# Two hypernetwork convolutions: new layout for the small network's variances, merging on ScalarE, another kind of weights last in each step, another order of transfers

## The chip, the cores and the metric

The program runs on one core of a Trainium2 chip. The metric is the device time of one execution in microseconds (us). The profile is of one execution, and its rows name the engines PE (TensorE), PEld (TensorE's weight loads), DVE (VectorE), ACT (ScalarE), POOL (GpSimd) and SP (SyncE, which here only issues DMAs). L586 is line 586 of the kernel before.

## The reference

x has the shape (32, 32, 64, 256): 32 samples s, 32 batches b, 64 channels, 256 places l. Two layers of the same form follow each other, each with its own parameters:

```python
# GroupNorm of each sample: 32 groups of 8 places l, each over b, channels and its places
xn = (x - mean) / sqrt(var + 1e-5)
# a small network makes a convolution of its own for every (b, l)
h  = relu(LN(z @ W1 + b1))                       # (32, 256, 128)
w  = (h @ W2 + b2).reshape(32, 256, 64, 64, 3)   # in, out, tap
hb = relu(LN(z @ Wb1 + bb1))                     # a second one for the bias
bias = (hb @ Wb2 + bb2)
out[s,b,o,l] = sum_ik xn[s,b,i,l+k-1] * w[b,l,i,o,k] + bias[b,o,l]
x = x + out
```

The group's statistics of layer 2 are those of layer 1's result. LN is the LayerNorm over the 128 hidden values; since z has 16 columns, its variance is a quadratic form in z (the matrix is called `form` in the kernel).

## The kernel before

**Units and steps.** A layer is worked in 32 units (4 quarters of the 256 places x 8 groups of 4 b's), a unit in two halves of 32 output channels. So the kernel has 128 steps v. In step v PE makes the weights of half a unit in 12 groups: `make` (L574, L575) multiplies the hidden values by 8 output channels' part of W2 into a PSUM tile `pg` (three buffers). The three kinds of groups (0, 1, 2) are the pairs of taps. `take` adds b2 and puts the result into the SBUF tile `wall`, of which there is one: kinds 0 and 1 with one add of DVE (L586, 128 partitions), kind 2 with an add of DVE for 64 partitions (L586, 64x1024) and eight of ACT for the other 64 (L597, one for each channel). `order` in the program lists the twelve: four times the kinds 2, 0, 1.

**Products.** `products(v)` multiplies the normalized x (`xn`) by `wall` (L621, 288 matmuls in four quarters into `pc`, two buffers), and DVE adds each quarter to the residual in `ring` (L630). In layer 1 DVE then takes the statistics of the new x (`bn_stats`, L314, two for each quarter) for layer 2. PE's order is written out: the first group of step v+1 is made ahead of `products(v)`, the other eleven behind it. Since `wall` is one tile, `products(v)` waits for the last `take` of step v, and the first `take` of step v+1 for `products(v)`.

**Around a step.** `after(v)` issues the transfers on SP: in layer 1 the pieces of x for the statistics of the next quarters (`land`, L664), the store of the result (L523), the residual of step v+2 (L186), hidden values (L141), the next half of x into `raw` (L170 or L179), which POOL normalizes (L560, twice 128x2112 for each half) and the bias (L511, four DMAs), which POOL adds to the residual (L518). `agenda` spreads the rest over the twelve places k of a step: DVE's `bn_stats` of the pieces (L671), and, when a quarter's statistics are complete, their merging (`Merge`, L331 to L356: eight operations of DVE, a matmul `over` L342, four of DVE, a second matmul, a root on ACT, a reciprocal on DVE). `Table` spreads mean and root over the partitions.

**First phase.** Ahead of step 1 the kernel takes the statistics of the first 11 of 32 groups (22 transfers of 1 MB, `bn_stats` L476 on DVE), and in between works the small networks for all units: 16 `Unit`s, two (hidden and bias net) for each of 8 pieces of z. For each, PE forms and sums the quadratic form (L248, L253) with the positions on the free axis, ACT takes relu and root of 128x512 (L254, L255), DVE the reciprocal of 128x512 (L256) and POOL multiplies (L257); then PE makes the hidden values (L267), ACT brings them out (L269) and sends them to DRAM (L279), and the bias net's go through PE once more (L289) and out (L298, L305). The twelve groups of step 0 are put among the last units, then come the merging, the table and the normalization of unit 0 on DVE (L560).

Of the kernel before, what the change touches and what calls it, by code (L numbers as in the profile page):

```python
# [23 lines left out]
FP = mybir.dt.float32  # L24
# [6 lines left out]
P = 128  # L31
# [8 lines left out]
PARAMS = ("z", "wc", "vec", "W2", "b2", "Wb2")  # L40
# [3 lines left out]
def conv_layers(  # L44
# [40 lines left out]
    hd = [dram.tile([2, P, 2 * M], FP, name=f"hd_{i}") for i in range(U // 2)]  # L85
# [18 lines left out]
    apart = const.tile([P, G], FP, name="apart")  # L104
# [33 lines left out]
    def load_hidden(i):  # L138

        h = hp.tile([P, 2, 2, M], FP, tag="hT", name="hT")  # L140
        nc.sync.dma_start(  # L141
            out=h.rearrange("p b a m -> p b (a m)"), in_=hd[i].rearrange("b p f -> p b f")
        )
        for b in range(2):
            hs[2 * i + b] = h[:, b]
# [44 lines left out]
    class Network:  # L190


        def __init__(self, stage, par, n):
# [10 lines left out]
            self.form = stage.tile([P, 2, P], FP, name=f"form_{n}")  # L204
            nc.gpsimd.memset(self.form, 0.0)

        def prepare(self, stage):
# [5 lines left out]
            for net in range(2):  # L213
# [6 lines left out]
                for r in range(0, P, R):  # L220
                    x = slice(r, r + R)
                    nc.vector.tensor_scalar(self.form[x, net, x], p2[x, x], 1.0 / P, None, ALU.mult)

    class Unit:


        def __init__(self, nets, zts, blocks, e):
            self.e, self.blocks = e, blocks
            self.j, self.net = divmod(e, 2)
            self.w = nets[self.j * NR // (UL // 2)]  # L230
            self.zt = zts[self.j % 2]
            flat = xn.rearrange("p n t j s -> p (n t j s)")
            self.q = flat[:, e % 3 * BLK : (e % 3 + 1) * BLK]
            o = 3 * BLK
            if self.net:
                o += 6 * BLK
                self.ht = [flat[:, o + k * 2 * BLK : o + (k + 1) * 2 * BLK] for k in range(2)]
            else:
                self.ht = [flat[:, o + x * 2 * BLK : o + (x + 1) * 2 * BLK] for x in ((e + k) % 3 for k in range(2))]
            o = 13 * BLK  # L240
            self.bs = [
                flat[:, o + k * BLK // 2 : o + (k + 1) * BLK // 2].rearrange("p (t a m) -> p t a m", t=NT, a=2)
                for k in range(3)
            ]

        def project(self):
            p = ps_c.tile([P, BLK], FP, tag="pc", name="pt")
            nc.tensor.matmul(p, self.w.form[:, self.net], self.zt, start=True, stop=True)  # L248
            nc.vector.tensor_tensor(self.q, self.zt, p, ALU.mult)
# [612 lines left out]
```

## Time and profile before

| | |
|---|---|
| three runs | 4101.36, 4085.76 and 4092.62 us, median 4092.62 us |
| the profiled execution | 4084.62 us, of it 4082.8 us in the span of the profile |
| busy, share of the span | PE 94%, PEld 90%, DVE 67%, POOL 47%, ACT 31% |
| granted TensorE clock, mean | 0.974 of full speed |
| first phase, to the last evacuation of step 0 | 250.06 us |
| step 1 | 39.16 us |
| steps 2 to 64 (the rest of layer 1 and the first of layer 2) | 1953.76 us, PE busy 1845.27 us |
| from there to the end | 1839.82 us, PE busy 1802.65 us |

The end of a step is read throughout as the start of the fourth L630 of its products: the moment at which PE has finished the products. A busy share says how full an engine is over a whole stretch. It doesn't say which wait ends last in a step, for which the rows with their idle times are needed: in brackets behind a row stands how long the engine idled ahead of it and what it waited for. "issue" there means that nothing in the profile shows what it waited for.

### The profile page before, as it was taken

The page shows a single profiled execution, that of the slowest core. Times are in us where ns is not written, and L with a number is a line of the kernel's source. Part 1 is how long each engine was busy: PE and PEld are TensorE (multiplying, and loading weights), DVE is VectorE, ACT ScalarE, POOL GpSimd, SP SyncE. Part 2 cuts the span into 40 slices and gives each one's busy share as a digit, 9 for nine tenths or more (in the row PEclk, how much of TensorE's full clock was granted, in tenths as well). Part 3 has the DMA queues.
Part 4 walks back from the last instruction along what each step waited for, and adds up shares of the span by engine and source line. Part 5 has one row for each costly group of instructions (what it writes and reads, how often), then busy time and mean ns, then how long its engine had stood idle before and what let it go on. Part 6 is the DMA issues. An engine that isn't in the chain of part 4 may idle for free.

```text
span 4082.8 us, 185286 instructions
## 1 busy us (share of the span) xinstructions
PE 3824.2 (94%) x86444; PEld 3655.0 (90%) x86444; DVE 2715.9 (67%) x3019; ACT 1276.0 (31%) x4320; POOL 1935.0 (47%) x629
## 2 busy tenths in 40 slices
PE   5669999799998999899998999999999999999999
PEld 1369999799987999899998999999999999999999
DVE  5677777777777777767676556565656565656565
ACT  3423333233222333233332323233323233323232
POOL 1143554434544445535545446654555455545542
PEclk6789999899999999999999999999999999999999
DMA  6565655455554554444457877787877787878783
GB/s 235 158 232 178 200 176 172 140 185 187 182 182 133 187 183 161 141 129 155 149 153 174 153 141 158 143 161 148 156 141 155 142 160 146 156 147 157 143 153 93
DMA packets 655906, 657.74 MB, mean 161 GB/s; under 512 B 563736, under 2 KB 587680, under 8 KB 589216
## 3 DMA queue, kind: packets, MB, share of 16 engines
q1 hardware_dynamic: 629024, 633.31, 62.4%
q8 instruction: 676, 11.08, 1.2%
q10 hardware_dynamic: 26112, 12.59, 1.1%
q14 instruction: 94, 0.77, 0.1%
HBM read 496.91 MB, written 148.90 MB: 158 GB/s over the span
## 4 chain that ended last, share of the span: by engine, by line
PE 85%; DVE 10%; issue 2%; DMA 1%; ACT 1%; ACTq 1%; POOL 0%; SPq 0%; DVEq 0%; POOLq 0%
PE pg L574 55%; PE pc L621 23%; PE pg L575 5%; DVE wall L586 4%; DVE parts L314 1%; DVE ring L630 1%; PE pt L248 0%; DMA ring<-in_xg_dram 0%; DVE first_parts L476 0%; DVE parts L335 0%; DMA land<-in_xg_dram 0%; ACTq L305 0%; DVE parts L334 0%; ACT wall L597 0%; DVE xn L256 0%
## 5 line engine op out<-in xcount | busy, mean ns | idle before, releaser
L574 PE MATMUL pg<-hT,w2t 128*64 128x128 f32 x24576 | 2755.1, 274 | 80.8 <-DVE wall L586 74.1
L574 PEld LDWEIGHTS pg<-hT,w2t 128*64 128x64 f32 x24576 | 2690.0, 137 | 124.3 <-DVE wall L586 90.8
L575 PE MATMUL pg<-hT,w2t 128*64 128x128 f32 x24576 | 2755.5, 274 | 1.3 <-issue 1.0
L575 PEld LDWEIGHTS pg<-hT,w2t 128*64 128x64 f32 x24576 | 2690.2, 137 | 1.6 <-issue 1.4
L586 DVE TENSOR_TENSOR wall<-pg,b 128x1024 f32<-128x1024 f32 (+1 forms) x1536 | 1861.1, 1219 | 604.3 <-PE pg L575 599.5
L597 ACT ACTIVATE wall<-pg,b 64x128 f32<-64x128 f32 x4096 | 1161.7, 474 | 2655.2 <-DVE wall L586 1939.5
L560 POOL TENSOR_TENSOR xn<-raw,tab 128x2112 f32<-128x2112 f32 x126 | 664.0, 5270 | 1591.5 <-PE pc L621 1398.4
L621 PE MATMUL pc<-wall,xn 128*32 128x128 f32 (+1 forms) x36864 | 960.5, 262 | 67.9 <-issue 59.3
L621 PEld LDWEIGHTS pc<-wall,xn 128*32 128x32 f32 x36864 | 913.4, 110 | 116.4 <-issue 108.4
L630 DVE TENSOR_TENSOR ring<-pc,ring 128x512 f32<-128x512 f32 x512 | 353.9, 691 | 658.7 <-PE pc L621 643.7
L518 POOL TENSOR_TENSOR ring<-ring,bt 128x2048 f32<-128x2048 f32 x127 | 580.0, 4567 | 41.8 <-DMA bt<-bd 33.5
L560 POOL TENSOR_TENSOR xn<-xn,tab 128x2112 f32<-128x2112 f32 x126 | 592.0, 4698 | 9.9
L314 DVE BATCH_NORM_STATS2 parts<-ring 128x6 f32<-128x256 f32 x512 | 192.9, 418 | 8.7
L671 DVE BATCH_NORM_STATS2 first_parts<-land 128x6 f32<-128x512 f32 x168 | 114.4, 681 | 8.4 <-DMA land<-in_xg_dram 8.4
L257 POOL TENSOR_TENSOR xn<-xn,zt 128x512 f32<-128x512 f32 x16 | 20.3, 1266 | 155.0 <-DVE xn L256 134.3
L554 POOL COPY raw<-edge 64x64 f32<-64x64 f32 x96 | 28.6, 298 | 137.1 <-DMA edge<-xe 134.8
L398 POOL COPY tab<-spot 64x1024 f32<-64x1024 f32 x28 | 29.0, 1035 | 129.7 <-ACT spot L385 128.8
L256 DVE RECIPROCAL xn<-xn 128x512 f32<-128x512 f32 x16 | 53.6, 3350 | 25.0 <-ACT xn L255 25.0
L289 PE MATMUL pb<-xn,Wb 128*64 128x256 f32 x128 | 29.0, 562 | 37.4 <-ACT xn L298 33.8
L289 PEld LDWEIGHTS pb<-xn,Wb 128*64 128x64 f32 x128 | 8.9, 180 | 57.9 <-ACT xn L298 45.1
L269 ACT ACTIVATE xn<-ph,vec 128x1024 f32<-128x1024 f32 x32 | 37.5, 1198 | 24.0 <-PE ph L267 14.7
L476 DVE BATCH_NORM_STATS2 first_parts<-ring 128x6 f32<-128x512 f32 x68 | 41.2, 668 | 4.8 <-DMA ring<-in_xg_dram 4.8
(81 smaller groups left out, 399.3 us busy)
## 6 DMA issues: line engine op xcount, KB each, us to landing
bt<-bd SPq DMA_DIRECT2D x508, 256.0 KB, 6.1
raw<-in_xp_dram SPq DMA_DIRECT2D x63, 1056.0 KB, 10.0
ring<-in_xs_dram SPq DMA_DIRECT2D x64, 1024.0 KB, 8.2
x<-ring SPq DMA_DIRECT2D x64, 1024.0 KB, 4.9
raw<-x SPq DMA_DIRECT2D x256, 256.0 KB, 7.9
ring<-x SPq DMA_DIRECT2D x64, 1024.0 KB, 9.4
out_dram<-ring SPq DMA_DIRECT2D x64, 1024.0 KB, 4.9
land<-in_xg_dram SPq DMA_DIRECT2D x48, 1024.0 KB, 5.1
```

The costliest lines, as they stand in the source:

```text
L256: nc.vector.reciprocal(self.q, self.q)
L314: nc.vector.bn_stats(out, y.rearrange("p o (a m) -> p o a m", a=2)[:, :, :, g * e : (g + 1) * e])
L476: nc.vector.bn_stats(first_parts[:, g, bg], slots[order[i]][:, k])
L518: nc.gpsimd.tensor_tensor(y, y, bts.pop(v), ALU.add)
L560: eng.tensor_tensor(o, i, tab[:, x, None, j0:j1].to_broadcast(list(o.shape)), op)
L574: nc.tensor.matmul(pg[0:C, k, :], w[:, k0 * C : (k0 + 1) * C], h0, start=True, stop=True)
L575: nc.tensor.matmul(pg[C:P, k, :], w[:, k1 * C : (k1 + 1) * C], h1, start=True, stop=True)
L586: nc.vector.tensor_tensor(place(rows, a), pg[rows].rearrange("p o (t m) -> p t m o", t=NT), b2[n][rows, kind, None, None, o0 : o0 + OG].to ...
L597: nc.scalar.activation(place(rows, a)[:, :, :, k], pg[rows, k].rearrange("p (t m) -> p t m", t=NT), AF.Identity, bias=b2[n][rows, kind, o0 ...
L621: nc.tensor.matmul(pc[t * S : (t + 1) * S, n0 - q * EB : n1 - q * EB, :], xn[:, u % 2, t, p, :], wall[:, t, a : a + (n1 - n0) * CH], start ...
L630: nc.vector.tensor_tensor(part, pc.rearrange("p (m a) o -> p o a m", a=2), part, ALU.add)
L671: nc.vector.bn_stats(first_parts[:, g, bg], lands[i % LAND])
```

## The change

The diff below is cut to its core; every part that the prediction speaks of is in it.

1. **Variances with positions on partitions.** `Batch` takes the place of `Unit`: eight of them, each for both nets and four units. The variance of a position becomes one number on a partition's row, so relu, root and reciprocal work on 128x32 instead of 128x512, once for both nets. New are a second layout of z as an input (`zp`), two multiplications of 128x256 and a reduction on DVE, and eight transposes with a copy of 128x1024 on ACT (`turn`).
2. **First phase.** The 22 transfers come in the order of groups; the merging of the first 9 groups starts after 18 of them, and the last two groups are merged in step 2.
3. **Merging on ScalarE.** Of the eight operations of DVE three reductions stay; scaling and squaring go to ACT (`around`), the rest is folded into the second matmul. `Table.expand` goes to POOL and `spread` one step later.
4. **Order of kinds.** The twelve groups of a step are four times 0, 1, 2. The last two `bn_stats` of `products` come behind the first `take` of the next step.
5. **Transfers of a step.** The store stands first, then the pieces, the residual, the bias (a step earlier than before) and the hidden values; the half of x is issued at k = 2.
6. **Two buffers for x.** From unit 24 on the second half of a unit goes to `land` instead of `raw`.

```diff
     class Batch:
...
+        def variance(self):
...
+            for x in range(2):
+                nc.vector.tensor_tensor(
+                    q[:, x], t[:, x, :, :, 0:A], zp[:, x, :, None, :].to_broadcast([P, 2 * NR, 2, A]), ALU.mult
+                )
+            nc.vector.tensor_reduce(self.var, self.q.rearrange("p (y a) -> p y a", a=A), AX.X, ALU.add)
+            var = self.var.rearrange("p (x r n) -> p x r n", x=2, n=2)
+            nc.vector.tensor_tensor(var, var, t[:, :, :, :, A], ALU.add)
+            nc.scalar.activation(self.var, self.var, AF.Relu)
+            nc.scalar.activation(self.var, self.var, AF.Sqrt, bias=eps)
         def scale(self):
-            nc.scalar.activation(self.q, p, AF.Relu)
-            nc.scalar.activation(self.q, self.q, AF.Sqrt, bias=eps)
-            nc.vector.reciprocal(self.q, self.q)
-            nc.gpsimd.tensor_tensor(self.q, self.q, self.zt, ALU.mult)
+            nc.vector.reciprocal(self.var, self.var)
...
+        def turn(self):
...
+            nc.scalar.copy(self.zq, p)
...
-        def merge(self):
...
-            nc.vector.tensor_reduce(m, means, AX.X, ALU.add)
-            nc.vector.tensor_scalar(m, m, 1.0 / shape[2], None, ALU.mult)
-            nc.vector.tensor_reduce(v, squares, AX.X, ALU.add)
-            nc.vector.tensor_tensor(means, means, m[:, :, None].to_broadcast(shape), ALU.subtract)
-            nc.vector.tensor_tensor(means, means, means, ALU.mult)
-            nc.vector.tensor_reduce(d, means, AX.X, ALU.add)
...
+        def sums(self):
+            nc.vector.tensor_reduce(self.m, self.means, AX.X, ALU.add)
+            nc.vector.tensor_reduce(self.v, self.squares, AX.X, ALU.add)
+        def around(self):
...
+            nc.scalar.activation(self.v, self.v, AF.Copy, scale=1.0 / N1)
+            for g in range(self.n):
+                nc.scalar.activation(self.means[:, g], self.means[:, g], AF.Square, bias=self.d[:, g : g + 1])
+        def spans(self):
+            nc.vector.tensor_reduce(self.d, self.means, AX.X, ALU.add)
...
-                if n == 0:
-                    for g in range(2 * q, 2 * q + 2):
-                        bn_stats(parts[:, g, bg, h, :], y, g)
+                if n == 0 and q < NB - 1:
+                    last_stats(v, q)
...
+        def place_half(u, k):
+            return land if k == 1 and u >= 3 * BG else raw
...
         def after(v):
             u, h = divmod(v, NH)
+            store(v)
             load_pieces(v + 1)
-            store(v)
             if v + 2 < NH * U:
                 load_residual(v + 2)
+                load_bias(v + 2)
             if h == 1 and u % 2 == 1 and u + 3 < U:
                 load_hidden((u + 3) // 2)
-            next_half(*((u + 1, 1) if h == 0 else (u + 2, 0)))
-            if v + 1 < NH * U:
-                next_bias(v + 1)
         starts = range(0, CH, OG)
-        order = [(kind, o) for o in starts for kind in (2, 0, 1)]
+        order = [(kind, o) for o in starts for kind in (0, 1, 2)]
...
         def agenda(v):
             todo = {k: [] for k in range(len(order))}
+            u, h = divmod(v - 1, NH)
+            todo[0].append(lambda: last_stats(v - 1))
+            todo[0].append(lambda: after(v - 1))
+            todo[2].append(lambda: next_half(*((u + 1, 1) if h == 0 else (u + 2, 0))))
+            if v + 1 < NH * U:
+                todo[5].append(lambda: add_bias(v + 1))
...
             for m in merges:
-                todo[2].append(m.merge)
-                todo[4].append(m.mean)
-                todo[6].append(m.root)
+                todo[2].append(m.sums)
+                todo[3].append(m.around)
+                todo[5].insert(0, m.spans)
+                todo[6].append(m.mean)
+                todo[8].append(m.root)
```

The next rows are the instructions of DVE around the products of a step in layer 2, in the order in which the built program has them (`wall<-pg` is `take`'s add, `ring<-pc` the addition of the products). Before:

```order
L586 TENSOR_TENSOR wall_205<-pg_32545,b2_1_228 64x128x8
L586 TENSOR_TENSOR wall_205<-pg_32571,b2_1_228 128x128x8
L586 TENSOR_TENSOR wall_205<-pg_32589,b2_1_228 128x128x8
L630 TENSOR_TENSOR ring_204<-pc_32624,ring_204 128x64x8
L630 TENSOR_TENSOR ring_204<-pc_32662,ring_204 128x64x8
L630 TENSOR_TENSOR ring_204<-pc_32700,ring_204 128x64x8
L630 TENSOR_TENSOR ring_204<-pc_32738,ring_204 128x64x8
L586 TENSOR_TENSOR wall_205<-pg_32607,b2_1_228 64x128x8
```

And the same place of the changed program (L646 is the add, L697 the addition of the products):

```order
L646 TENSOR_TENSOR wall_205<-pg_33948,b2_1_228 128x128x8
L646 TENSOR_TENSOR wall_205<-pg_33966,b2_1_228 128x128x8
L646 TENSOR_TENSOR wall_205<-pg_33984,b2_1_228 64x128x8
L697 TENSOR_TENSOR ring_204<-pc_34027,ring_204 128x64x8
L697 TENSOR_TENSOR ring_204<-pc_34065,ring_204 128x64x8
L697 TENSOR_TENSOR ring_204<-pc_34103,ring_204 128x64x8
L697 TENSOR_TENSOR ring_204<-pc_34141,ring_204 128x64x8
L646 TENSOR_TENSOR wall_205<-pg_34010,b2_1_228 128x128x8
```

The add of 64 partitions, behind which ACT's eight follow, stood third from the last ahead of the products; now it is the last.

The transfers that SP issues in two steps of layer 2 (`x1` is layer 1's result, `bd` the bias, `hd` the hidden values, `xe` the edges). Before:

```order
L523 DMA out_0_dram<-ring_204 128x2048
L186 DMA ring_204<-x1_18_90 128x2048
L141 DMA hT_43685<-hd_26_162 128x2x256
L179 DMA raw_202<-x1_19_91 32x64x32 x4
L511 DMA bt_43696<-bd_25_193 32x2048 x4
L523 DMA out_0_dram<-ring_204 128x2048
L186 DMA ring_204<-x1_19_91 128x2048
L161 DMA edge_44107<-xe_12_116 64x128
L163 DMA edge_44107<-xe_28_132 64x128
L179 DMA raw_202<-x1_20_92 32x64x32 x4
L511 DMA bt_44115<-bd_25_193 32x2048 x4
```

Now:

```order
L583 DMA out_0_dram<-ring_204 128x2048
L184 DMA ring_204<-x1_18_90 128x2048
L571 DMA bt_43828<-bd_25_193 32x2048 x4
L141 DMA hT_43833<-hd_26_162 128x512
L177 DMA land_203<-x1_19_91 32x64x32 x4
L583 DMA out_0_dram<-ring_204 128x2048
L184 DMA ring_204<-x1_19_91 128x2048
L571 DMA bt_44246<-bd_25_193 32x2048 x4
L159 DMA edge_44299<-xe_12_116 64x128
L161 DMA edge_44299<-xe_28_132 64x128
L177 DMA raw_202<-x1_20_92 32x64x32 x4
```

The four bias transfers went from behind the half of x to ahead of it, and the half of a unit's second part goes to `land`.

In the first phase DVE's row for one pair of units was, word for word from the built program before:

```order
L249 TENSOR_TENSOR xn<-zt_234,pt 128x512
L256 RECIPROCAL xn<-xn 128x512
L476 BN_STATS first_parts<-ring 128x6 x4
L249 TENSOR_TENSOR xn<-zt_236,pt 128x512
L256 RECIPROCAL xn<-xn 128x512
L476 BN_STATS first_parts<-ring 128x6 x4
```

And it is, for one batch:

```order
L461 BN_STATS first_parts<-ring 128x6 x2
L259 TENSOR_TENSOR xn<-pt,zp_235 128x256 x2
L262 TENSOR_REDUCE xn<-xn 128x32
L264 TENSOR_TENSOR xn<-xn,pt 128x32
L461 BN_STATS first_parts<-ring 128x6 x2
L269 RECIPROCAL xn<-xn 128x32
L646 TENSOR_TENSOR wall<-pg,b_0_227 128x128x8
L461 BN_STATS first_parts<-ring 128x6 x4
```

The two reciprocals of 128x512 and the two long multiplications are replaced by two multiplications of 128x256, a reduction, an add of 128x32 and a reciprocal of 128x32.

## Rows read from the trace of the kernel before

**Rows 1.** The chain that ended last: share of the span by engine.

```profile
PE 85%; DVE 10%; issue 2%; DMA 1%; ACT 1%; ACTq 1%; POOL 0%; SPq 0%; DVEq 0%; POOLq 0%
```

**Rows 2.** Windows: stretch, length, busy time and instructions by engine, granted clock, DMA share, GB/s.

```profile
0.00:250.06 250.06, 145.60 (x1046) 73.34 (x1048) 160.63 (x208) 88.30 (x139) 36.94 (x37) 0.72 0.63 206
250.06:289.22 39.16, 30.69 (x674) 29.55 (x674) 22.28 (x28) 9.38 (x33) 21.59 (x8) 0.91 0.67 221
289.22:2242.98 1953.76, 1845.27 (x42414) 1784.41 (x42414) 1438.19 (x1770) 604.54 (x2126) 920.15 (x260) 0.98 0.54 167
2242.98:4082.80 1839.82, 1802.65 (x42316) 1767.67 (x42314) 1094.79 (x1015) 573.74 (x2022) 956.37 (x326) 1.00 0.76 147
```

**Rows 3.** Windows of single steps, and of steps 50 to 61 together.

```profile
320.43:349.13 28.70, 28.52 (x675) 28.02 (x676) 22.27 (x28) 9.37 (x33) 0.01 (x1) 1.00 0.57 187
...
1784.65:2134.87 350.22, 347.23 (x8076) 337.54 (x8076) 242.64 (x290) 114.87 (x404) 173.93 (x57) 1.00 0.51 151
...
2711.57:2739.85 28.28, 28.28 (x674) 28.02 (x675) 17.34 (x16) 9.06 (x32) 7.05 (x4) 1.00 0.84 154
```

**Rows 4.** Waits from 300 to 2150 us: total, times, longest.

```profile
PE pg L574 <- DVE wall L586: 58.6, 60, 18.5
...
PE pc L621 <- issue: 22.7, 30, 1.8
```

**Rows 5.** Waits from 2250 to 4070 us.

```profile
PE pc L621 <- issue: 28.6, 48, 2.3
```

**Rows 6.** Timeline of DVE, layer 2: start, duration, instruction, idle time before it.

```profile
2759.17 1.23 DVE L586 TENSOR_TENSOR wall<-pg,b 128x1024 f32<-128x1024 f32 x1 [0.52 <-PE pg L575]
...
2803.53 1.22 DVE L586 TENSOR_TENSOR wall<-pg,b 64x1024 f32<-64x1024 f32 x1 [0.52 <-PE pg L575]
```

**Rows 7.** Timeline of PE at four places.

```profile
127.21 0.32 PE L574 MATMUL pg<-hT,w2t 128*64 128x128 f32 x1 [0.98 <-ACT wall L597]
...
2162.83 0.53 PE L621 MATMUL pc<-wall,xn 128*32 128x128 f32 x12 [1.90 <-issue]
...
2195.16 4.00 PE L621 MATMUL pc<-wall,xn 128*32 128x128 f32 x104 [3.83 <-issue]
...
2760.80 1.07 PE L621 MATMUL pc<-wall,xn 128*32 128x64 f32 x34
```

**Rows 8.** Timeline of ACT, first phase and layer 2.

```profile
62.69 2.30 ACT L269 ACTIVATE xn<-ph,vec 128x1024 f32<-128x1024 f32 x2 [0.67 <-PE ph L267]
...
73.39 0.47 ACT L298 ACTIVATE xn<-pb,vec 128x256 f32<-128x256 f32 x1 [1.02 <-DMA ring<-in_xg_dram]
73.89 1.28 ACTq L305 DMA_DIRECT2D bd<-xn  x2
...
124.91 2.25 ACT L597 ACTIVATE wall<-pg,b 64x128 f32<-64x128 f32 x8 [1.35 <-DVE wall L586]
...
2804.84 2.26 ACT L597 ACTIVATE wall<-pg,b 64x128 f32<-64x128 f32 x8 [2.50 <-DVE wall L586]
```

**Rows 9.** Windows behind the second and third of the waits in rows 7.

```profile
2162.83:2167.00 4.17, 3.99 (x130) 3.65 (x132) 2.18 (x5) 0.00 (x0) 4.05 (x3) 1.00 0.44 178
2194.58:2197.99 3.41, 2.83 (x64) 2.68 (x68) 1.45 (x3) 0.00 (x0) 0.00 (x0) 0.50 1.01 416
```

**Rows 10.** Timeline of DVE in the merging of step 16.

```profile
713.63 0.51 DVE L331 TENSOR_REDUCE moments<-parts 128x8 f32<-128x256 f32 x1
714.17 4.10 DVE L332 TENSOR_SCALAR moments<-moments 128x8 f32<-128x8 f32 x1
```

**Rows 11.** Timeline of POOL at the same time.

```profile
713.59 4.66 POOL L560 TENSOR_TENSOR xn<-xn,tab 128x2112 f32<-128x2112 f32 x1
```

**Rows 12.** Timeline of DVE in the first phase.

```profile
57.82 0.69 DVE L249 TENSOR_TENSOR xn<-zt,pt 128x512 f32<-128x512 f32 x1 [6.26 <-PE pt L248]
...
79.84 0.69 DVE L249 TENSOR_TENSOR xn<-zt,pt 128x512 f32<-128x512 f32 x1 [5.93 <-PE pt L248]
...
215.82 2.47 DVE L476 BATCH_NORM_STATS2 first_parts<-ring 128x6 f32<-128x512 f32 x4 [4.75 <-DMA ring<-in_xg_dram]
```

More of the change, by code (lines that the diff above doesn't have):

```diff
@@ new lines, in spans, with over @@
+        def spans(self):
+            nc.vector.tensor_reduce(self.d, self.means, AX.X, ALU.add)
+        def over(self, *xs):
+            ps = ps_c.tile([P, 2, G], FP, tag="pc", name="over")
+            for i, x in enumerate(xs):
+                nc.tensor.matmul(
+                    ps[:, 0, 0 : self.n],
+                    same.rearrange("p t s -> p (t s)"),
+                    x,
+                    start=(i == 0),
+                    stop=(i == len(xs) - 1),
+                )
+            return ps[:, :, 0 : self.n]
@@ L450, in first_phase @@
                 load_b2(n)
+            stats(0, range(LAND))
+            nets[0].prepare(stage)
+            count = U // 2 // NR
             made = {}
[L452 to L468 removed]
@@ L470, in first_phase @@
-            for i in range(units):
-                if i == 4:
-                    nets[1].prepare(stage)
-                step(i)
-                for k in range(LAND):
-                    bg, g = divmod(i * LAND + k, FIRST[0])
-                    nc.vector.bn_stats(first_parts[:, g, bg], slots[order[i]][:, k])
-                for k in after[i]:
-                    load(k)
-                if i == 3:
-                    load_w2(0, 0, CH)
-                if i == 6:
+            begins = {1 + 2 * j: j for j in range(count)}
@@ new lines, in begun @@
+            def begun(i):
+                j = begins.get(i)
+                return None if j is None else made[j]
+            for i in range(1, units):
+                b = begun(i - 3)
+                if b:
+                    for k in range(NR):
+                        b.bias(k)
+                b = begun(i - 2)
+                if b:
+                    b.hidden(0)
+                    b.hidden(1)
+                b = begun(i - 1)
+                if b:
+                    b.turn()
+                if i in begins:
+                    made[begins[i]] = Batch(nets, zts, zps, zs, begins[i])
+                b = begun(i)
+                if b:
+                    b.form()
+                if i == needed:
+                    merge = Merge(first_parts.rearrange("p g b f -> p g (b f)")[:, 0 : GT + 1], 0, 0)
+                    table = Table(0)
+                    merge.sums()
+                    merge.around()
+                if i == needed + 1:
+                    merge.mean()
+                    add_bias(0)
+                    merge.root()
+                    table.expand(nc.vector)
+                stats(i, range(2))
+                if b:
+                    b.variance()
+                if i == needed:
+                    merge.spans()
+                stats(i, range(2, LAND))
+                if b:
+                    b.scale()
+                    load_z(b.j + 2)
+                if i == 2:
+                    load_w2(0, 0, CH)
+                if i == 3:
+                    nets[1].prepare(stage)
+                if i == 5:
```

279 lines of the change are left out of this document (140 added, 139 removed).

## The prediction

> **What bounds the kernel now.** I read the chain of work that ended last first, then the windows by stage, then single steps. TensorE makes up 85% of the chain [rows 1], and the windows show where it is not full [rows 2]: in the first phase it works 145.6 of 250.06 us, in step 1 30.7 of 39.16, in steps 2 to 64 1845 of 1954 and afterwards 1803 of 1840. So there are two kinds of time. In layer 2 a step without a wait lasts 28.28 us, all of it TensorE [rows 3]; nothing that relieves another engine can shorten it, and each microsecond that TensorE is made to wait is a microsecond of the total. In layer 1 a step without a wait lasts 28.70, the mean of twelve steps without merging is 350.22/12 = 29.19 [rows 3], and 63 such steps would be 1838.7. The stretch of steps 2 to 64 lasts 1953.8 [rows 2], so 115 us are lost beyond that. The waits name the place: PE waits for VectorE's add L586, 58.6 us in 60 times, the longest 18.5 [rows 4]. The timeline of one merging shows why: the reduction L331 takes 0.51 us, but the scaling of eight numbers in L332 takes 4.10 [rows 10] and ends as POOL's multiplication ends, 713.59 + 4.66 = 718.25 [rows 11]. Several operations in a row are held like this while the adds stand behind them.
>
> **The change, part by part.** The sum is made against the profiled execution, 4082.8 us of span and 1.8 around it.
>
> *Kinds 0, 1, 2 (the largest term).* The products wait for the last `take`. Before, that was an add of VectorE for all 128 partitions: it starts at 2759.17 and PE's products at 2760.80 [rows 6, 7], 1.63 us later; in that time PE makes the next step's first group, so it hardly waits. Now the last `take` is kind 2: the add of 64 partitions, which takes just as long (1.22 at 2803.53), and only then ACT's eight operations (start 2804.84, 2.26 us, so end 2807.10) [rows 6, 8]. That is 3.57 us from the add's start. ACT hands over to PE within 0.05: 124.91 + 2.25 = 127.16, PE at 127.21 [rows 7, 8]. The products start 3.62 instead of 1.63 later, and PE has nothing to fill the gap, as `make` of the second group stands behind the products in its order. That is 2.0 us for each of 126 steps (63 in each layer), 252 us; the first step after the first phase I carry in its own term. The bounds: 0.7 if ACT's operations started together with the add (2.26 + 0.05 - 1.63), and 2.2 if the hand-over to products, whose first matmul waits for VectorE and ACT both, takes four times the 0.05. I take 2.0, the row's own value. What is late next is everything behind the products: the L630 additions, the first `take` of the next step, SP's store; all move with PE and none of them ends later relative to it.
>
> *The last two statistics behind the first `take` (layer 1).* A step without waits has 28.70 in layer 1 and 28.28 in layer 2 [rows 3]; the difference is what VectorE's statistics do to TensorE. With the two last ones moved behind the add, I take all of the 0.42 as gone: 63 x 0.42 = -27. Bounds: 0 and -27.
>
> *Merging on ScalarE.* Three reductions remain on VectorE; the row shows that this kind isn't held (0.51) [rows 10]. Eleven short operations move to ACT, which is busy 9.4 of 28.7 us in a step [rows 3] and has room between two of its `take`s. Of the 115 us I let 14.5 stay: eight mergings at 0.7 (three reductions of 0.51 less VectorE's idle 0.52 ahead of each add [rows 6]) and 9 for the steps in which layer 1 hands over to layer 2. That is -100; bounds -70 and -110. If the cover goes, that is if ACT's `take`s are late by the short operations, 11 of them at about the 0.3 of one of the eight in L597 (2.26/8 [rows 8]) make 3.3 us for each merging, 26 in all.
>
> *First phase.* Two units of the small networks now take 79.84 - 57.82 = 22.0 us [rows 12]. ACT's own work for a batch is 2 x 2.30 (hidden) + 4 x 0.47 and 4 x 1.28 (bias out and its DMAs) [rows 8], and one copy like L269's half, 1.15: 12.8 us. Between 12.8 and 22.0 I choose 20, near today's, because bias products and ACT still go in turns. Seven periods at 2.0 less are 14. The four transfers that the first merging no longer waits for bring 4 x 2.47 of statistics, and the wait for the last transfer, 4.75 [rows 12], goes: 14.6. Together -28, so that step 0's last evacuation comes at 222. Bounds: 0 and -60.
>
> *Transfers, two buffers, step 1.* Step 1 has 39.16 with 30.7 of TensorE [rows 2]; what it waits for is the load of the pieces for its statistics, which now comes once and first. I take 32, its own 2.0 included: -7. In later steps transfers are hidden by the step's length before and after: the DMA share is 0.84 and 0.57 in steps in which PE doesn't wait [rows 3]. I cost the new order at nothing; without cover a late half of x would hold POOL's normalization, which has a step to spare.
>
> *Waits without a cause ("issue") ahead of products.* In layer 2 they are 28.6 us in 48 times [rows 5], in layer 1 22.7 in 30 [rows 4]. They fall in the products, that is behind the new wait. If PE's sequencer is late with its instructions there, 2.0 us of rest in each step give it time; I take two thirds of layer 2's as gone, -18, and none of layer 1's. Bounds: 0 and -50. The Trainium skill (Runtime: NRT & Kernel Launch, Instruction fetch mechanics) has it that instructions are fetched while the engine works and that crossing a block is "mostly hidden"; by it these waits would be something else and would stay, and the sum would be 18 higher. The rows, 1.8 and 2.3 us at the longest, show something that isn't hidden, and do not say what it is.
>
> The sum: 252 - 27 - 100 - 28 - 7 - 18 = +72. So 4084.6 + 72 = 4156 for an execution like the profiled one. The median of the three runs is 8 above the profiled one; I give 4160, between 4156 and 4164.
>
> **Rivals.** (1) *The clock falls in the new waits.* After 1.90 us without work the clock stayed at 1.00 (2.4 GHz), after 3.83 it was at 0.50 (1.2 GHz) for 3.41 us [rows 7, 9]. The new wait of 2.0 lies just above the first. Each fall costs half of 3.41, 1.7 us. If it comes in a third of the steps, 42 x 1.7 = +71, so 4231; in all, 4374. For it: the wait comes in every step; against it: the row of 1.90. (2) *The waits without a cause stay*: 4178. (3) *The first phase is no shorter*, since ACT and its DMAs set the pace as before: 4188. (4) *Faster.* The new wait would be small if ACT's operations didn't wait for the add of the same group: then the products start 2.31 behind its start, 0.7 more than the 1.63 of now, and 126 x 0.7 = 88 instead of 252, so 3996. The point from which it decides is 72/126 = 0.57 less in each step, a wait of 1.43. Against it stands that ACT starts 0.09 behind the add's end wherever its idle time is put down to L586 [rows 6, 8]. (5) *Nothing visible.* The wait is 1.4 to 1.5, or the first phase gives 60 and the waits without a cause all go: 4156 - 32 - 32 = 4092.
>
> **How the numbers follow.** Forecast 0.60 (its own range 4120 to 4190), the clock 0.12, waits that stay 0.10, first phase no shorter 0.06, faster 0.05, nothing visible 0.07. A measurement of this kernel can tell about 0.5%, 20 us, from no change. The range from 4095 to 4235 takes in cases 2, 3, most of the forecast and the part of case 1 in which the clock falls in up to a third of the steps; left out are the faster case, full falls of the clock and half of case 5. Faster by over 0.5%: 0.06, within 0.5%: 0.10, slower: 0.84.
>
> **What would show it.** In the profile after: a wait of PE's products for ACT's L657 of about 2.0 us, some 126 times, is the main term; if the rows name VectorE's add and 0.7, case 4 holds. A step of layer 2 without other waits should last 30.3 us, one of layer 1 30.3 to 30.7. The windows behind the waits should have the clock at 1.00; 0.5 there is case 1. Merging steps should be within 2 us of their neighbours, with no 4 us operations among VectorE's. Step 0's last evacuation should come at 222, with reciprocals of 128x32 instead of 128x512. The waits without a cause should fall in layer 2 from 28.6 to about 10. I would be wrong above all if something in PE's order fills the wait, or if the merging finds another operation that POOL holds.

## The result and the profile after

The changed kernel takes 4260.59 us (median of 4 runs, 4258.26 to 4265.69) beside 4096.99 for the kernel before on the same chips: a ratio of 1.0402, 95% interval 1.0371 to 1.0433. It is slower, as forecast, but by 4.0% instead of the 1.8% of the sum, and it lies above the range. The profiled execution has a span of 4263.9 us.

The windows of the changed kernel answer to [rows 2] (length, then busy time of PE, PEld, DVE, ACT, POOL, granted clock, DMA share, GB/s):

```profile
0.00:271.28 271.28, 150.03 (x1114) 96.06 (x1116) 107.89 (x208) 83.07 (x146) 33.93 (x50) 0.79 0.60 193
271.28:303.14 31.86, 29.31 (x674) 28.02 (x674) 22.14 (x28) 9.34 (x33) 21.36 (x8) 1.00 0.72 214
303.14:2290.83 1987.69, 1836.84 (x42450) 1786.74 (x42450) 1363.61 (x1710) 623.11 (x2230) 915.87 (x265) 1.00 0.56 165
2290.83:4263.90 1973.07, 1810.90 (x42316) 1772.87 (x42316) 1092.62 (x1009) 572.57 (x2022) 964.25 (x335) 1.00 0.73 137
```

Against the rows of before, the first phase is 21 longer (271.28 for 250.06), step 1 is 7 shorter, steps 2 to 64 are 34 longer and the rest is 133 longer: +181. My sum had -28, -7, -1 and +108, which is +72. So step 1 was right, and 49, 35 and 25 us are missing in the three other stretches. The mean clock of each window is 1.00 from step 1 on. In steps 2 to 126 it stands at 0.50 (1.2 GHz) for two stretches of 3.41 us, behind waits of 2.44 and 2.31 us.

The wait that I took for the largest term is there, in its size. In the timeline of VectorE in step 111 the last add, now that of 64 partitions, starts at 3746.31:

```profile
3746.31 1.22 DVE L646 TENSOR_TENSOR wall<-pg,b 64x1024 f32<-64x1024 f32 x1 [0.52 <-PE pg L635]
```

ACT's eight operations follow in its own timeline:

```profile
3747.62 2.25 ACT L657 ACTIVATE wall<-pg,b 64x128 f32<-64x128 f32 x8 [2.97 <-DVE wall L646]
```

And PE's products start behind them, in this step and in the next:

```profile
3749.92 0.43 PE L688 MATMUL pc<-wall,xn 128*32 128x64 f32 x12 [1.92 <-ACT wall L657]
...
3782.73 0.54 PE L688 MATMUL pc<-wall,xn 128*32 128x64 f32 x16 [1.96 <-issue]
```

From the add's start to the products' start it is 3.61 us (3.62 was forecast; 1.63 before). In 49 of the 126 steps the row puts the idle time down to "issue" instead of ACT, with 1.95 at the median. The idle time ahead of the first product of each step adds up to 123.0 us in steps 2 to 64 and 123.4 afterwards, where it was 0.0 and 1.4.

A merging of the changed kernel, in the timelines of POOL (first row) and VectorE, answers to [rows 10]: three reductions and a reciprocal, none of them held, though POOL has a long multiplication at the time of the first two.

```profile
749.24 4.69 POOL L620 TENSOR_TENSOR xn<-xn,tab 128x2112 f32<-128x2112 f32 x1
...
749.29 0.49 DVE L357 TENSOR_REDUCE moments<-parts 128x8 f32<-128x256 f32 x1
...
749.71 0.48 DVE L358 TENSOR_REDUCE moments<-parts 128x8 f32<-128x256 f32 x1
...
754.94 0.49 DVE L369 TENSOR_REDUCE apart<-parts 128x8 f32<-128x256 f32 x1
...
763.32 0.21 DVE L394 RECIPROCAL moments<-over 128x8 f32<-128x8 f32 x1 [2.60 <-ACT over L393]
```

Two things are new. In the waits of the first phase (20 to 271 us; total, times, longest) ACT waits for the bias transfers, for which it waited only 5.0 us in the kernel before:

```profile
ACT xn L328 <- DMA bd<-xn: 44.2, 10, 7.6
```

And PE's waits from 2320 to 3950 us show that in layer 2 it now waits without a cause inside the weights (L634, L635), where it hardly did before:

```profile
PE pc L688 <- ACT wall L657: 55.5, 29, 2.0
PE pc L688 <- issue: 48.5, 34, 2.0
PE pg L635 <- issue: 12.6, 13, 1.7
PE pg L634 <- issue: 10.2, 13, 2.0
```

### The profile page after: what moved, and what is told of

It is laid out like the page before. It is cut to its first block, busy times and chain, and to the rows that moved or that the text cites. A ratio compares the mean times of both kernels' runs of the same rounds, so it can differ in the third digit from the quotient of the medians.

```text
span 4263.9 us, 185545 instructions
## 1 busy us (share of the span) xinstructions
PE 3827.1 (90%) x86548; PEld 3683.7 (86%) x86548; DVE 2586.3 (61%) x2954; ACT 1288.1 (30%) x4431; POOL 1935.4 (45%) x655
## 4 chain that ended last, share of the span: by engine, by line
PE 74%; DMA 4%; ACT 4%; issue 4%; DVE 3%; POOL 2%; SPq 1%; ACTq 0%; POOLq 0%
PE pg L634 45%; PE pc L688 22%; PE pg L635 7%; DMA bt<-bd 4%; ACT wall L657 4%; DVE wall L646 3%; POOL ring L578 2%; SPq L571 1%; SPq L184 0%; DVE ring L697 0%; PE spread L419 0%; SPq L728 0%; SPq L583 0%; PE pe L598 0%; DVE first_parts L735 0%
## 5 line engine op out<-in xcount | busy, mean ns | idle before, releaser
L634 PE MATMUL pg<-hT,w2t 128*64 128x128 f32 x24576 | 2750.5, 274 | 28.9 <-issue 19.3
L635 PE MATMUL pg<-hT,w2t 128*64 128x128 f32 x24576 | 2752.7, 274 | 18.0 <-issue 17.6
L634 PEld LDWEIGHTS pg<-hT,w2t 128*64 128x64 f32 x24576 | 2687.2, 137 | 61.4 <-issue 39.3
L635 PEld LDWEIGHTS pg<-hT,w2t 128*64 128x64 f32 x24576 | 2686.9, 137 | 25.4 <-issue 24.8
L646 DVE TENSOR_TENSOR wall<-pg,b 128x1024 f32<-128x1024 f32 (+1 forms) x1536 | 1871.9, 1219 | 687.0 <-PE pg L635 681.2
L697 DVE TENSOR_TENSOR ring<-pc,ring 128x512 f32<-128x512 f32 x512 | 353.9, 691 | 843.3 <-PE pc L688 843.3
L620 POOL TENSOR_TENSOR xn<-raw,tab 128x2112 f32<-128x2112 f32 x86 | 438.9, 5104 | 568.0 <-PE pc L688 521.7
L620 POOL TENSOR_TENSOR xn<-land,tab 128x2112 f32<-128x2112 f32 x40 | 224.7, 5617 | 106.4 <-DMA land<-x 106.2
L593 ACT COPY rim<-ring 128x64 f32<-128x64 f32 x64 | 19.5, 305 | 532.6 <-DVE ring L697 516.2
L274 POOL TENSOR_TENSOR raw<-zp,xn 128x256 f32<-128x256 f32 x16 | 10.3, 644 | 173.5 <-DVE xn L269 82.9
L298 PE MATMUL ph<-xn,wc 17*128 17x512 f32 x128 | 41.3, 1061 | 39.1 <-ACT xn L288 37.7
L298 PEld LDWEIGHTS ph<-xn,wc 17*128 17x128 f32 x128 | 12.6, 295 | 58.2 <-ACT xn L288 39.7
L259 DVE TENSOR_TENSOR xn<-pt,zp 128x256 f32<-128x256 f32 x16 | 6.0, 419 | 74.6 <-PE pt L246 74.6
```

Source lines behind the costliest of these rows:

```text
L298: nc.tensor.matmul(p[:, r], self.w.wc[x, net], self.zq[x, net], start=True, stop=True)
L620: eng.tensor_tensor(o, i, tab[:, x, None, j0:j1].to_broadcast(list(o.shape)), op)
L634: nc.tensor.matmul(pg[0:C, k, :], w[:, k0 * C : (k0 + 1) * C], h0, start=True, stop=True)
L635: nc.tensor.matmul(pg[C:P, k, :], w[:, k1 * C : (k1 + 1) * C], h1, start=True, stop=True)
L646: nc.vector.tensor_tensor(place(rows, a), pg[rows].rearrange("p o (t m) -> p t m o", t=NT), b2[n][rows, kind, None, None, o0 : o0 + OG].to ...
L697: nc.vector.tensor_tensor(part, pc.rearrange("p (m a) o -> p o a m", a=2), part, ALU.add)
```

## The experiments

The expectations below speak of instruction blocks. In the trace a DMA queue of the kind "instruction" moves 677 packets of 16384 bytes. PE has 173096 matmuls and weight loads in the changed kernel, some 256 for each of these packets, so I take the packets for PE's program, which comes in blocks while it runs.

Twelve kernels were run. The table gives for each the stretches that matter and, for layer 2, the sum of PE's idle times ahead of the first product of a step, ahead of the other products, and ahead of the weights' matmuls (added up from the timeline of PE between the fourth additions of steps 64 and 127). us is the median; the kernel before had 4088.49, 4098.47 and 4089.39 beside the first, second and third four. All stretches are of one profiled execution, and the stretch of layer 2 differs by 11 to 13 us between kernels that have the same program there (changed and e3, e1 and e7). Totals of different groups are less sure by what the kernel before differs, up to 10 us.

| kernel | us | ratio (95%) | step 0 ends | steps 2-64 | layer 2 | first | other products | weights |
|---|---|---|---|---|---|---|---|---|
| before | 4097.0 | 1 | 250.1 | 1953.8 | 1834.2 | 1.4 | 29.4 | 0.7 |
| changed | 4260.6 | 1.040 (1.037-1.043) | 271.3 | 1987.7 | 1967.6 | 123.4 | 5.2 | 28.1 |
| e1 kinds 2,0,1 | 4017.3 | 0.983 (0.981-0.985) | 265.9 | 1880.5 | 1832.3 | 1.4 | 7.5 | 17.5 |
| e2 two groups ahead | 4093.2 | 1.001 (0.999-1.002) | 266.1 | 1909.5 | 1873.9 | 15.3 | 5.9 | 29.8 |
| e3 four bias buffers | 4231.4 | 1.036 (1.034-1.038) | 242.4 | 1987.5 | 1956.9 | 124.1 | 5.5 | 19.3 |
| e4 transfers as before | 4246.6 | 1.040 (1.038-1.041) | 267.3 | 1997.1 | 1937.6 | 124.3 | 5.5 | 0.5 |
| e5 before, merging on ACT | 4036.1 | 0.986 (0.982-0.989) | 251.5 | 1886.3 | 1846.5 | 1.4 | 35.9 | 1.6 |
| e6 statistics inside | 4263.5 | 1.041 (1.038-1.044) | 266.2 | 1996.0 | 1964.6 | 123.4 | 5.5 | 23.2 |
| e7 e1 and e3 | 4007.4 | 0.979 (0.977-0.981) | 243.8 | 1880.5 | 1845.1 | 1.4 | 13.9 | 18.9 |
| e8 e7, transfers as before | 4042.5 | 0.987 (0.985-0.989) | 240.8 | 1915.4 | 1846.7 | 1.4 | 33.4 | 2.3 |
| e9 bias behind the half | 4204.9 | 1.028 (1.026-1.030) | 263.7 | 1974.8 | 1930.3 | 123.8 | 5.1 | 0.8 |
| e10 half of x early | 4259.7 | 1.042 (1.040-1.044) | 271.3 | 1992.7 | 1961.5 | 123.5 | 3.9 | 22.0 |
| e11 blocks shifted | 4248.1 (one run) | - | 264.3 | 1988.8 | 1955.8 | 124.5 | 5.9 | 15.1 |
| e12 e7, bias behind the half | 3972.7 | 0.971 (0.970-0.973) | 239.5 | 1866.6 | 1838.8 | 1.4 | 30.3 | 1.1 |

**e1.** The order of the kinds undone.

```diff
-        order = [(kind, o) for o in starts for kind in (0, 1, 2)]
+        order = [(kind, o) for o in starts for kind in (2, 0, 1)]
```

> The changed kernel with the order of kinds 2, 0, 1 as before; everything else is as changed. Theory (the wait for ACT's eight operations behind the last add is the whole cost of the order): PE's first product of a step waits 0 to 0.1 us instead of 1.95, 126 steps give back 246 us, so about 4261 - 246 = 4015, some 2% faster than the kernel before. Rival (the wait only shows at this place, and PE would wait elsewhere for the same late work): the time stays above 4150 and the waits appear ahead of the weights' matmuls.

4017.34 us, 2 from what the theory said: the order of the kinds alone costs 243 us (234 if the two ratios are compared). PE's waits from 2320 to 3950 us no longer have ACT in them:

```profile
PE pg L635 <- issue: 7.9, 14, 1.1
PE pc L688 <- issue: 7.0, 19, 0.7
PE pg L634 <- issue: 7.0, 11, 1.1
```

**e2.** The order 0, 1, 2 kept, and the second group of weights made ahead of the products too.

```diff
-                weights(v, k, (lambda: products(v - 1)) if k == 0 else None)
+            pgs = [make(hs[v // NH], order[k][0], v % NH * CH + order[k][1]) for k in range(2)]
+            products(v - 1)
...
+                weights(v, k, pgs[k] if k < 2 else None)
```

> The changed kernel, order of kinds 0, 1, 2, but PE makes two groups of the next step ahead of the products instead of one. Theory (the wait is ACT's tail, 1.95 us, and PE has nothing to fill it): a second group of 1.75 us fills it, 0.2 is left, so about 4261 - 126 x 1.75 = 4040. Rival (the products wait for something else that ends at the same time, as a POOL addition or a transfer): the wait moves with it and the time stays within 30 us of 4261.

The wait goes from 1.95 to 0.2 as the theory said, and the rest of it is put down to ACT:

```profile
PE pc L688 <- ACT wall L657: 9.8, 48, 0.3
```

But of the 220 us only 167 came: the shortest step of layer 2 is 28.79, not 28.28 + 0.24 = 28.52, and steps in layer 1 are 0.8 above those of e1 (29.34 for 28.58). So a second group ahead of the products has a price of its own. Where it arises isn't shown.

**e3.** The change had also gone from three buffers for the bias net's results to two, a line which my diff had cut.

```diff
-            self.bs = [take(BLK // 2).rearrange("p (t a m) -> p t a m", t=NT, a=2) for _ in range(2)]
+            spare = tab.rearrange("p x j s -> p (x j s)")
+            self.bs = [
+                spare[:, k * BLK // 2 : (k + 1) * BLK // 2].rearrange("p (t a m) -> p t a m", t=NT, a=2)
+                for k in range(NR)
+            ]
```

> The changed kernel with four buffers for the bias net's results in the first phase (in the table's space, which is not yet used) instead of two. Theory (ACT waits for the bias transfers of two pieces earlier because there are only two buffers, some 46 us in eight batches): step 0 ends at 225 to 240 us instead of 271, the total is 30 to 46 lower, 4215 to 4231. Rival (the turn-taking of PE, ACT and POOL in a batch sets the pace): step 0 ends above 260, the total is within 10 of 4261.

Step 0 ends at 242.4 instead of 271.3, 2 us behind the theory's latest, and the total is 29 lower (18 by the ratios). The waits of its first phase (20 to 242 us) show what went and what stayed:

```profile
DVE apart L373 <- ACT first_parts L370: 13.3, 1, 13.3
...
ACT tab L332 <- DMA bd<-tab: 7.3, 3, 2.6
```

44.2 us of ACT's waits for the bias transfers are down to 7.3; the two buffers were the cause. How much they cost is less sure: the other kernels with two buffers end step 0 between 263.7 and 271.3, and e7 against e1 gives 22. The first row is the next bound: ACT's part of the merging stands behind the last batch's bias work in ACT's order, and VectorE waits 13.3 for it.

**e4.** The transfers of a step as before; the half of x and the addition of the bias move with them, and the table's `spread` one place forward.

```diff
+            load_pieces(v + 1)
             store(v)
-            load_pieces(v + 1)
             if v + 2 < NH * U:
                 load_residual(v + 2)
-                load_bias(v + 2)
...
+            next_half(*((u + 1, 1) if h == 0 else (u + 2, 0)))
+            if v + 1 < NH * U:
+                add_bias(v + 1)
+            if v + 2 < NH * U:
+                load_bias(v + 2)
```

> The changed kernel with the transfers of a step in the order of before (pieces, store, residual, hidden values, half of x, bias), the half of x and the bias being issued at the first place of the step. Theory (the waits without a cause are late instruction blocks, whose place is set by where a block ends in the program, not by the order of the transfers): total within 15 us of 4261, such waits 45 to 65 us in all as in both kernels. Rival (the new order puts more transfers against the instruction blocks in the weights' part of the step): these waits leave the weights' matmuls, layer 2 gains some 26 us, about 4235.

The rival holds for layer 2: the waits inside the weights are gone and it is 30 us shorter. PE's waits from 2320 to 3950 us:

```profile
PE pc L688 <- ACT wall L657: 57.7, 30, 1.9
PE pc L688 <- issue: 50.0, 29, 2.2
...
PE pg L634 <- issue: 0.3, 1, 0.3
```

In layer 1 and step 1 it lost 9 and 3 again, so the total moved only 14 (3 by the ratios). By the total alone the theory would stand; the waits decide against it. The clock bears on the loss: in steps 2 to 126 of this run it stands at 0.50 for 3.41 us 16 times, in the changed kernel twice. Eleven of the 16 stand behind waits of 1.97 or 1.98 us ahead of the products. One of them, in PE's timeline and in the windows:

```profile
2535.40 0.56 PE L688 MATMUL pc<-wall,xn 128*32 128x64 f32 x9 [1.98 <-issue]
...
2535.47:2538.88 3.41, 3.41 (x77) 3.41 (x81) 0.00 (x0) 0.00 (x0) 3.33 (x2) 0.50 0.00 0
```

At half of 3.41 us each, as in the prediction, the eight additional ones in steps 2 to 64 make an estimated 14 us, and the six in layer 2 make 10.

**e5.** The kernel before with the classes `Merge` of the changed kernel.

```diff
-                todo[2].append(m.merge)
-                todo[4].append(m.mean)
-                todo[6].append(m.root)
+                todo[2].append(m.sums)
+                todo[3].append(m.around)
+                todo[5].insert(0, m.spans)
+                todo[6].append(m.mean)
+                todo[8].append(m.root)
```

> The kernel before with the merging on ScalarE alone (three reductions stay on VectorE; Table.expand stays on VectorE, one place later). Theory (VectorE's short operations with operands in SBUF alone are held until POOL's long ones end, and that is what merging steps lose): steps 2 to 64 go from 1954 to about 1875, total about 4090 - 80 = 4010. Rival (merging steps lose their time to transfers or to the matmuls between): less than 30 gained, total above 4060.

Steps 2 to 64 are 67 us shorter, the total 62, nearer to the theory than to the rival. VectorE's rows in the merging of step 16 stand beside [rows 10], where the step lasted 53.03; it lasts 31.75 here.

```profile
712.93 0.49 DVE L327 TENSOR_REDUCE moments<-parts 128x8 f32<-128x256 f32 x1
713.35 0.49 DVE L328 TENSOR_REDUCE moments<-parts 128x8 f32<-128x256 f32 x1
```

Steps 16, 32 and 48 give 21, 21 and 13 us, those at 63 and 64 together 12; those at 13 and 29 only 1.5 and 1.4, and every merging step is still 2 to 5 above its neighbours.

**e6.** The last two statistics back in `products`.

```diff
-                if n == 0 and q < NB - 1:
+                if n == 0:
...
-            todo[0].append(lambda: last_stats(v - 1))
```

> The changed kernel with the last two statistics back inside the products, ahead of the first take. Theory (they cost TensorE 0.4 us in each step of layer 1, and moving them saved that): a step of layer 1 without other waits lasts 30.7 instead of 30.28, steps 2 to 64 are some 25 longer, total about 4286. Rival (the backlog of VectorE is used up elsewhere in the step): the shortest steps stay at 30.28 and the total at 4261.

The theory falls: the shortest step of layer 1 stays at 30.27 and the total within 3 us. Of the 0.38 by which the shortest step is below before's 28.70 once the new wait of 1.95 is taken off, nothing is due to the moved statistics here. With kinds 2, 0, 1 and the statistics moved (e1) it is 28.58, so there the move can give about 0.1 at most.

**e7.** e1 and e3 together, with no other edit.

> The changed kernel with kinds 2, 0, 1 and four bias buffers: both found costs taken out. Theory (they add up): 4017 - 28 = 3989, step 0 at 238, faster than both kernels. Rival (without the wait in the first phase something else sets its end, since step 0 came 5 us earlier already with kinds 2, 0, 1): 4005 to 4017.

4007.41 lies in the rival's range, 18 above the theory. The rival's reason doesn't hold all the same: step 0 ends 22 earlier than in e1. In the profiled execution layer 2 was 13 longer, with the same program there.

**e8.** e7 with e4's edit.

> As the kernel with kinds 2, 0, 1 and four bias buffers, with the transfers of a step in the order of before. Theory (the old order frees the weights' matmuls from late instruction blocks, but without the 2 us of rest ahead of the products the late blocks fall into the products again, as in the kernel before): layer 2 stays at 1832 within 6 us, total 3985 to 4000. Rival (the order of transfers alone makes the difference of 30 us that layer 2 showed): layer 2 about 1803, total about 3960.

Neither range holds: layer 2 lasted 1846.7, 9 above the theory's upper end but as in e7 (1845.1), and the total lies 42 above it. What the theory said of the place of the waits is seen: without the rest they are in the products again, 33.4 us. The total was 35 higher than e7, since steps 2 to 64 lost 35: PE waits inside the products there for 48.8 us in all, which e7 hasn't (14.0). I had not expected that and haven't followed it up.

**e9.** The four bias transfers issued behind the half of x.

```diff
-                load_bias(v + 2)
...
+                todo[2].append(lambda: load_bias(v + 1))
                 todo[5].append(lambda: add_bias(v + 1))
```

> The changed kernel with the four bias transfers issued behind the half of x (place 2) instead of ahead of it. In layer 2 PE's waits inside the weights are 28 us with the new order and 0.5 with the old one. Theory (the bias ahead of the half pushes the half's many small packets into the part of the step in which an instruction block is due): these waits fall under 8 us and layer 2 from 1968 to about 1945. Rival (it is the later place of the half): they stay over 18 us, layer 2 above 1958.

Layer 2 is 37 us shorter than with the change, 15 more than the theory asked for, and the waits inside the weights are 0.8:

```profile
PE pc L688 <- ACT wall L657: 57.6, 30, 2.0
PE pc L688 <- issue: 51.3, 35, 2.0
PE pg L635 <- issue: 0.4, 1, 0.4
```

**e10.** The half of x at the first place of the step, still behind the bias; the table's `spread` again moves with it.

```diff
-            todo[2].append(lambda: next_half(*((u + 1, 1) if h == 0 else (u + 2, 0))))
+            todo[0].append(lambda: next_half(*((u + 1, 1) if h == 0 else (u + 2, 0))))
```

> The changed kernel with the half of x issued at the first place of the step, but still behind the bias. Theory (the bias ahead of the half matters): PE's waits inside the weights of layer 2 stay over 18 us, since the half's packets still come last. Rival (the later place of the half matters): they fall under 8 us, layer 2 to about 1945.

No difference to the change (22.0 us of waits in the weights); with e9, in which only the four bias transfers move, this shows that the bias ahead of the half is the cause, not the half's place:

```profile
PE pg L634 <- issue: 9.5, 14, 2.0
PE pg L635 <- issue: 8.3, 10, 2.3
```

**e11.** 32 more matmuls at the start of PE's program.

> The changed kernel with 32 more matmuls of 128x128 at the start of TensorE's program (their result is not used), which shift every later instruction by about half an instruction block; some 10 us more in the first phase. Theory (the order of transfers decides how many blocks are late, and as a step has no whole number of blocks all shifts occur anyway): PE's waits without a cause in layer 2 stay at 25 to 40 us in all, most of them in the weights. Rival (where the blocks' ends lie decides): their sum changes by more than 15 us or moves back into the products.

21.0 us of waits without a cause instead of 33.3, 15.1 of them in the weights: under the 25 that the theory asked for, but not the change of 15 that would show the rival. It is a single run, and e3, e6 and e10, which leave PE's program as it is and keep the bias ahead, have 24.8, 28.7 and 25.9. So a share of the blocks' place isn't shown, nor is it excluded.

**e12.** e7 with e9's edit.

> Kinds 2, 0, 1, four bias buffers, and the bias transfers behind the half of x. Theory (without the rest of 2 us ahead of the products blocks that are not late in the weights are late in the products): within 10 us of 4007. Rival (the order alone saves the late blocks): layer 2 about 20 us less than 1845, total about 3987.

3972.7 us, 2.9% less than the kernel before and the fastest of all. In layer 2 the waits went where the theory said (30.3 us in the products, 1.1 in the weights), with about the same sum as in e7 (31.4 for 32.8). The total is lower all the same, by 35 (31 by the ratios), outside the theory's 10 and below the rival's 3987. The profiled execution shows 14 of it in steps 2 to 64, where the waits ahead of the weights' matmuls fall from 16.1 to 6.9, 6 in layer 2 and 4 in the first phase; the rest is not accounted for.

## Why the prediction was right and wrong

**The kinds (+252) was right.** Place, cause and size: 246 us of waits ahead of the first products, 243 given back in e1. The rival of a falling clock did not come: of the two falls in steps 2 to 126 none stands behind one of the 112 waits of 1.9 to 2.0 us. But it was near. In e4, with the same wait ahead of the products, the clock fell behind eleven of them. The rival in which ACT doesn't wait for the add is out too.

**First phase (-28), wrong in sign: +21.** The step that failed is "Between 12.8 and 22.0 I choose 20, near today's". I had counted ACT's work and not the buffers behind it. The variances on 128x32 did take VectorE's work away (its busy time fell from 160.6 to 107.9), but VectorE wasn't what set the pace. With two buffers a batch takes (191.83 - 68.87)/5 = 24.6 us in VectorE's rows of L259, with four (e3, there L263) (174.19 - 64.84)/5 = 21.9, today's 22.0. The rows are the third and the last batch of each:

```profile
68.87 0.76 DVE L259 TENSOR_TENSOR xn<-pt,zp 128x256 f32<-128x256 f32 x2 [18.47 <-PE pt L246]
...
191.83 0.75 DVE L259 TENSOR_TENSOR xn<-pt,zp 128x256 f32<-128x256 f32 x2 [14.49 <-PE pt L246]
...
64.84 0.76 DVE L263 TENSOR_TENSOR xn<-pt,zp 128x256 f32<-128x256 f32 x2 [14.15 <-PE pt L250]
...
174.19 0.76 DVE L263 TENSOR_TENSOR xn<-pt,zp 128x256 f32<-128x256 f32 x2 [8.86 <-PE pt L250]
```

So 22 to 29 of the 49 missing us are the buffers. The others are the period that doesn't shrink (7 x 2.0 = 14 were counted) and, as far as e3's wait of 13.3 tells, the merging behind the last batch's bias; no run tests this last part.

**Merging (-100), too large: -67.** The mechanism was right: e5 shows the gain with this part of the change alone, and the rows of before and after show the operations that were held and that aren't any more. The mis-sized term is the 115 us that I took for the loss of merging steps. They were measured against twelve of the quietest steps, and only 97 of the 115 stand in steps 13, 16, 17, 29, 32, 48, 63 and 64; the others belong to ordinary steps, nearly all of them ahead of step 48, and e5 has as much there. Merging steps keep 2 to 5 us each, not 0.7. (The 0.7 doesn't come out of its own terms either: 3 x 0.51 - 0.52 is 1.0, over eight mergings 2 us more.)

**The statistics (-27).** e6 shows no effect of the move. The shortest step of layer 1 did fall by 0.38, but from the order of the kinds: a first `take` of one add frees its buffer sooner than one with ACT's operations behind it. That is argued from e1 and e6, not shown by itself. Over 63 steps it would be 24 us, about what is left when e5's 67 and the wait's 123 are set against the 34 by which steps 2 to 64 grew. So the gain that I had counted here came, but by luck, from another part of the change.

**Step 1 (-7) was right** in size (31.9 for 32). No run takes its cause apart.

**Transfers (0), wrong: 19 to 37 us in layer 2** (e4 and e9, 1937.6 and 1930.3, against the changed kernel, e3 and e6, 1956.9 to 1967.6). The step that failed is "I cost the new order at nothing". I had asked whether the data come in time, and they do; what comes late is instructions. A late one can be seen at step 112. PE's timeline:

```profile
3776.41 0.27 PE L634 MATMUL pg<-hT,w2t 128*64 128x128 f32 x1 [2.02 <-issue]
```

The queues' part of the DMA view, for 3773.0 to 3775.2 us, has one packet of the instruction queue among 1965 small ones:

```profile
DMA packets 1966, 0.27 MB, mean 121 GB/s; under 512 B 1965, under 2 KB 1965, under 8 KB 1965
...
q1 hardware_dynamic: 1965, 0.25, 104.8%
q8 instruction: 1, 0.02, 4.2%
```

In the trace's packets that block runs from 3773.14 to 3774.64, and starts 8.8 us after the start of the block before it. Of all waits of PE over 0.25 us that are put down to "issue" and don't stand ahead of a first product (73 in the kernel before from step 2 on, 72 in the changed one), the middle one ends 1.4 to 1.5 us after an instruction packet's end, and eight in ten lie between 1.3 and 1.6. Of PE's instructions at large one in twenty starts that long after such an end. So these waits are for instructions. In the changed kernel's layer 2 the late blocks are as quick as the others once they run (1.34 us at the median, the others 1.26), but they start 8.5 us after the start of the block before, the others 5.3: what is late is their start. With the bias ahead, the small packets of the half of x run later in the step, from 12.8 to 21.9 us after its beginning in nine of ten, and blocks come late in the weights. With the bias behind (e4, e9) they run from 8.0 to 16.9 and blocks don't come late there. What holds the start up, and why the place in the step matters, stays open.

**Waits without a cause in the products (-18): the number came, the reason only in part.** 29.4 us became 5.2, and all seven kernels with the rest of 2 us have 3.9 to 5.9 there. But e1 has the new order of transfers and no rest, and 7.5; e2, with 0.2 us of rest, has 5.9. In e7, without a rest too, it is 13.9. So under the new order most of these waits leave the products without any rest, and the forecast's reason isn't shown for this kernel. It does hold with the bias behind the half of x: e8 has no rest and 33.4 us, e4 the rest and 5.5; e12 has 30.3 and e9 5.1. For the sum the rival "they stay" holds: 28.1 came back in the weights. With both, the rest and the bias behind, the sum over layer 2 is 6 us (e4, e9); with one of them or none it is 21 to 37.5. Of the Trainium skill's sentence in Runtime: NRT & Kernel Launch (Instruction fetch mechanics), that crossing a block is mostly hidden, the trace agrees in so far as most of 5.3 blocks in each step (677 packets of the instruction queue for 128 steps) cause no wait; the waits left in layer 2, 6 to 37.5 us by kernel, are what isn't hidden.

The range was too narrow. Merging and statistics were set at or near their favourable ends, the first phase ended outside its bounds, the transfers had no bounds, and merging, first phase and transfers all missed to the same side. None of the five cases of the forecast was the one that came.

## What to carry to other kernels

Look which engine does the last piece ahead of a hand-over, not how busy it is: a tail of 2.25 us on an engine that is 31% busy cost 6% here, and undoing one tuple gave that back. When a change moves work off an engine, check what it takes in exchange, buffers above all: with two for the bias net's results step 0 ended 21 us later than before, with four (e3) 8 earlier. And the order of transfers is to be judged by everything on those queues, the instructions too: putting the bias behind the half of x gained 31 to 35 us in the best version (e7 to e12) without any change to an engine's work. In layer 2, though, it moved the waits there rather than ending them (31.4 us for 32.8).

## What the runs showed of the hardware

Instruction blocks come by a DMA queue of their own, and PE waits up to 2.4 us for one in layer 2 (e5) while nothing in its semaphores is open. Those waits move: with the bias behind the half of x, 2 us of rest ahead of the products takes them out of the products (33.4 to 5.5 us in layer 2 from e8 to e4, 30.3 to 5.1 from e12 to e9), and with the bias ahead they come in the weights (28.1 us in the changed kernel, 0.8 in e9). Idle times of 1.9 to 2.0 us ahead of the products left the granted clock at 1.00 in all 112 cases of the changed kernel, but not in every kernel: in e4 eleven of 1.97 or 1.98 us were followed by 3.41 us at 0.50.
